# Two recurrent layers on one core: the second layer's first group of input products in the two-level scheme, after the first layer's third group, with other places in the queues

## The chip, the cores and the metric

One Trainium2 chip, one of its cores. The engines of the core work side by side, each on its own queue in order: TensorE (PE, matrix products), VectorE (DVE), ScalarE (ACT), GpSimd (POOL) and SyncE (SP, which only issues DMAs). The metric is the device time of one execution in microseconds (us). Before the change the median of three runs was 1619.63 us (1619.02 to 1619.73); less is better.

## The reference, cut to what matters

Two recurrent layers run over 128 steps, each followed by a residual addition. The batch is 128 rows, a row has 512 features, everything is float32.

```python
def _L0_cond_ref(h_t, z, W, b, alpha):
    Wh = W[:, :D]; Wz = W[:, D:]; leak = 1.0 - alpha
    def step(h, z_t):
        gate = jax.nn.sigmoid(h @ Wh.T + z_t @ Wz.T + b)
        h_new = jnp.tanh(h * leak + gate * z_t)
        return (h_new, h_new)
    ...
def _L1_cond_ref(x, h0, Wx, Wh, b):
    xw = jnp.einsum('ntd,dh->nth', x, Wx) + b
    def step(prev_h, xw_t):
        next_h = jnp.tanh(xw_t + prev_h @ Wh)
        return (next_h, next_h)
    ...
x = x + _L0_cond_ref(cond_1024, x, L0_cond_W, L0_cond_b, L0_cond_alpha)
x = x + _L1_cond_ref(x, cond_1024, L1_cond_Wx, L1_cond_Wh, L1_cond_b)
```

The state products `h @ Wh` come one step after the other. The input products `z @ Wz` and `x @ Wx` do not depend on the state, so they can be formed for many steps at once.

## The kernel before, in words

**Tiling.** Features lie on the 128 partitions in four chunks, the batch of 128 in the free dimension. Layer 0 is "a" in the names of tiles, layer 1 is "b". Layer 1 runs `LAG` = 13 steps behind layer 0, in the same loop: step t holds layer 0's step t and layer 1's step t - 13. A state product of one half of the features (`state_product`, L424) is eight matmuls of 128 columns; a step of both layers has four such halves.

**Input products.** They are formed for groups of 8 steps (`B`) in Strassen's scheme in Winograd's form. On one level (the cases in `FLAT`) a group is 7 products ("outer" 1 to 7) of 4 matmuls with 512 columns, L344. On two levels each of the 7 is split again into 7 leaves: 49 matmuls with 256 columns, L350, in two sweeps, 4 leaves for each outer product in sweep 0 and 3 in sweep 1 (`INNER`). Before the change layer 0's first full group ("a", 1) and layer 1's first group ("b", 0) are on one level, and all later groups are on two.

**What a two-level group needs.** (1) Sums of inputs `S56`, `S73` (`add_up`, on POOL, 8 operations). (2) Nested sums of these, tiles `N12`, `N56`, `N73`, `N4` and `D...` (`nest`, on DVE, 16 operations L210). (3) Combined weights, "leaves": formed once by POOL (`combine_leaves`), written to DRAM (`keep_leaves`, four DMAs for each outer product), and streamed back through ten buffers by SP (`stream`, one DMA for each outer product and sweep, 256 KB or 192 KB; tiles `wsa`, `wsb`). (4) After each outer product `collect` (L371 on ACT for the first use of a part, L373 on DVE for the others) takes it out of its PSUM set (`A` or `B`), since the next but one outer product accumulates into the same set. (5) Between the sweeps eight additions (`gather`, L379, on DVE). Seeds for the state products are then copied into PSUM by ACT (`seed`, L413).

**The plan.** The program is written by a planner in the kernel's own code. `spread` gives each outer product a step, `shape_of` sets the order within a step, and a clock with a fixed cost for each piece gives every PE instruction a time. Everything else is then placed on a lane (DVE, ACT, POOL, SP) at the first free time after what it needs (`place`, `task`, `issue`), and the program is recorded in the order of these times. Each engine executes its queue strictly in that order, and what was placed late by the plan stands late in the queue whatever the real times are.

**x and the results.** A step's x comes by four DMAs on SP (`load_x`, L98), is turned by DVE (`prepare_x`, L168) into one of the T tiles, and a finished step is turned back (`to_natural`, L173) and stored by four DMAs on SP (`store`, L103). There are five x buffers and three o buffers. In a step of layer 0, ACT forms the gate (L471), DVE multiplies and adds (`mix0`, L477 and L480), ACT takes the tanh (L485), POOL adds the residual (L488); layer 1's tanh is L497 on ACT.

**Lines that the change and the prediction touch.** `FLAT` L200, `make` L238, `nest` L305, `set_of` L324, `part` L355, the spreads L531 to L546, `shape_of` L548, the loop over steps L572, the loads of x L786 to L791, the combined weights L794 to L803, the sums of groups L816 to L852, the fills L854 to L870.

Of the kernel before, what the change touches and what calls it, by code (L numbers as in the profile page):

```python
# [43 lines left out]
def kernel(  # L44
# [18 lines left out]
    G = 4  # L63
# [135 lines left out]
    FRESH = 1, 2, 5  # L199
    FLAT = {("a", "flat"): 2, ("a", 1): 4, ("b", 0): 4}  # L200

# [24 lines left out]
    class Layer:  # L226
# [11 lines left out]
        def make(self, what):  # L238
            pool, tag, shape = {"w": (tpool, "T", [P, C, C, P]), "wc": (bpool, "A1", [P, 4, 2, 2, P])}[what]
            setattr(self, what, pool.tile(shape, F32, tag=tag, name=f"{what}{self.name}"))  # L240

# [62 lines left out]

        def nest(self, key, pair, which):  # L305
            n = 1 if pair == "4" else 2
            if (key, pair) not in self.inner:
                self.inner[key, pair] = npool.tile([P, n, 3, 2 * P], F32, tag="N", name=f"N{pair}{self.name}_{key}")
                self.third[key, pair] = dpool.tile([P, n, 2 * P], F32, tag=f"D{pair}", bufs=1 if pair == "4" else 2, name=f"D{pair}{self.name}_{key}")
            i, d = self.inner[key, pair], self.third[key, pair]  # L310
            sums(
                nc.vector, lambda j: d if j == 3 else i[:, :, j - 5],
                lambda b, a: self.quarter(key, pair, b, a), which,
            )
# [9 lines left out]
        def set_of(self, key, sweep, outer):  # L324
            turned = (self.name, key) == ("a", 1) or ((self.name, key) not in FLAT and sweep == 0)
            return "AB"[(outer in (2, 5, 3)) != turned]
# [28 lines left out]
        def part(self, key, i):  # L355
            if key == "flat":
                if key not in self.parts:
                    self.parts[key] = bpool.tile([P, 2, 4, 2 * P], F32, tag="A1", name="Aflat")
                return self.parts[key][:, :, 2 * i : 2 * i + 2]
            if (key, i) not in self.parts:  # L360
                pool, tag = (apool, f"A0{self.name}") if i == 0 else (bpool, "A1")
                self.parts[key, i] = pool.tile([P, 2, 4, 2 * P], F32, tag=tag, name=f"A{i}{self.name}_{key}")
            return self.parts[key, i]
# [166 lines left out]

    spread(2, L0, 1, [(0, 1)], [(0, 2)], [(0, 6)], [(0, 5)], [(0, 3)], [(0, 7)], [(0, 4)])  # L531
    LOOSE = (
# [6 lines left out]
    )  # L539
    for g in range(NB):  # L540
        if g:
            spread(B * g + B, L1, g, *(LOOSE if g == NB - 1 else STEADY))
        else:
            spread(B, L1, 0, [(0, 1)], [(0, 2), (0, 6)], [(0, 5)], [(0, 7), (0, 3)], [(0, 4)])
        if 2 <= g:
            spread(B * g - G, L0, g, *STEADY)  # L546

    def shape_of(t, n):  # L548

        first = ["0", "0"] if t < T else []  # L550
        second = ["1", "1"] if LAG <= t < T + LAG else []
        if not n:
            return first + second
        if t == T:
            return ["u"] + second + ["u"] * (n - 1)
        if t % B < G or not second or not first:
            if t % G == 2 and second and first:
                return first + ["1", "u", "1"] + ["u"] * (n - 1)
            return first + second + ["u"] * n
        if t % G == 2:  # L560
            return first + ["1", "u", "1"] + ["u"] * (n - 1)
        if t % B == B - 1:
            return first + ["u"] * (n - 1) + second + ["u"]
        if t % G == 3:
            return first + ["u"] * n + second
        return first + ["u"] * min(n, 2) + second + ["u"] * max(0, n - 2)
# [3 lines left out]
    start = []  # L570
    clock = BEGIN
    for t in range(T + LAG):  # L572
        start.append(clock)
        left_ = list(units[t])
        halves = {"0": 0, "1": 0}
        u = t - LAG
# [3 lines left out]
        for kind in shape_of(t, len(left_)):  # L580
            if kind == "u":
# [4 lines left out]
                pe[layer.name, key, s, o] = clock  # L586
            elif kind == "0":
                i = halves["0"]
                halves["0"] += 1
                at(clock, L0.state_product, t, i, h0)  # L590
                clock += HALF
                pe["0", t, i] = clock
# [26 lines left out]
    done = {}  # L619
    VEC, LAT = 0.08, 0.065  # L620

# [19 lines left out]
    lanes.take("DVE", 0.0, 25.6)  # L641
    lanes.take("ACT", 0.0, 25.6)


# [87 lines left out]
    for u in range(T):  # L732
        for i in range(2):
# [4 lines left out]
            if u % B == 0:  # L738
                needs += [("c", "b", u // B, 1 if u else 0, 3 if i else 2)]
            task(("seed1", u, i), needs, "ACT", 0.3, 0.39, L1.seed, u, i)  # L740
        if u < T - 1:
            task(("res1", u), [("tanh1", u, 0), ("tanh1", u, 1)], "POOL", 1.27, 1.3, residual, u, h1)
    for key_ in list(pe):
        if len(key_) == 4:
# [3 lines left out]
            if s == 0 and o in COPIED:  # L748
                task(("c", *key_), [("pe", *key_)], "ACT", 0.09 + 0.00083 * n, 0.18 + 0.00083 * n, layer.collect, key, s, o)
            else:  # L750
                task(("c", *key_), [("pe", *key_)], "DVE", *vec(n), layer.collect, key, s, o)
# [9 lines left out]

    def nested_sums(layer, key, what, ok, outers):
        if len(pairs_done) >= 2:
            ok = max(ok, pairs_done[-2] + 0.1)
        occ, dur = vec(256 if what == "4" else 512)
        e = {}
        for which in (5, 7, 6, 3):
            r = max(ok, e.get(5, 0) if which == 6 else 0, e.get(6, 0) if which == 3 else 0) + LAT
            e[which] = place(
                ("N", layer.name, key, what, which), "DVE", r, occ, dur, layer.nest, key, what, which,  # L770
                apart=True,
            )
        pairs_done.append(max(begun[layer.name, key, 0, o] + UNIT[0] for o in outers))
# [12 lines left out]
    for t in turn:  # L786
        if t == 2 * B:
            issue(start[2] + 1.0, 4, load_w1, wx1, "wx")
        landed = issue(max(freed.pop(0) + 0.05, start[max(0, t - 15)] if t > 15 else 0.0), 4, load_x, t) + (5.0 if t < 2 * B else 2.9)
        e = place(("x", t), "DVE", max(landed, start[t - 12] + 0.3 if t >= 2 * B else 0.0), 0.7, 0.71, prepare_x, t)  # L790
        freed.append(e)  # L791


    lanes.take("POOL", 0.0, start[0])  # L794
    issue(start[4] + 1.0, 4, load_w1, wh1, "wh1")
    at(start[3] + 2.0, L1.make, "w")
    for kc in range(C):
        place(("wx", kc), "ACT", start[3] + 2.1, 0.6, 0.7, permute_w1, lambda: L1.w, "wx", kc)
        place(("wh", kc), "ACT", start[7] + 1.0, 0.6, 0.7, permute_w1, lambda: L1.wh, "wh1", kc)
    at(start[7] - 0.02, L1.make, "wc")  # L800
    e = start[7]
    for i in (5, 6, 7, 4):
        e = place(("wc", i), "POOL", e, 1.25, 1.3, L1.combine_weights, i, nc.gpsimd)  # L803

# [11 lines left out]
    for time, name, key in groups:  # L816
        layer = {"a": L0, "b": L1}[name]
        if name == "a":
            have = {t: done["x", t] for t in range(8 * key, 8 * key + 8)}
# [10 lines left out]
        for which, ok in ((5, high), (6, max(high, low)), (7, max(high, low)), (3, low)):  # L830
            for k in range(2):
                ready_ = max(ok, late[PAIR[which][0]] + 0.1, e.get(6, 0.0) if which == 3 else 0.0, e.get(5, 0.0) if which == 6 else 0.0)
                name_ = "S", name, key, which, k
                if (name, key) == ("b", NB - 1):
                    e[which] = place(name_, "DVE", ready_ + LAT, *vec(512), layer.add_up, key, which, nc.vector, k)
                else:
                    e[which] = place(
# [15 lines left out]

    for f in sorted(fill, key=lambda f: f[0]):  # L854
        _, kind, layer, key, what, ok, outers = f
        if kind == 0:
            nested_sums(layer, key, what, ok, outers)
        else:
            occ, dur = vec(512)
            r = ok + LAT  # L860
            for n in range(4):
                name_ = "G", layer.name, key, what, n
                r = place(name_, "DVE", r, occ, dur, layer.gather, key, what, n, nc.vector, apart=True) + 0.04

    for n, o in enumerate((6, 5, 7, 4, 1, 2, 3)):
        e = place(("leaves", o), "POOL", start[0] + 4.0 * n, 1.9, 2.0, L0.combine_leaves, o, nc.gpsimd)
        issue(e + 0.1, 4, L0.keep_leaves, o, nc.sync)
    for n, o in enumerate((6, 5, 7, 4, 1, 2, 3)):
        e = place(("leaves1", o), "POOL", max(e, start[8]), 1.9, 2.0, L1.combine_leaves, o, nc.gpsimd)
        issue(e + 0.1, 4, L1.keep_leaves, o, nc.sync)  # L870

# [41 lines left out]
```

## Time and profile before

| what | value |
|---|---|
| median of three runs | 1619.63 us (1619.02 to 1619.73) |
| the profiled execution | 1619.68 us |
| its span, first to last instruction | 1617.9 us |
| DVE busy | 1197.8 us (74%), 2054 instructions |
| ACT busy | 714.2 us (44%), 1923 instructions |
| POOL busy | 712.7 us (44%), 581 instructions |
| layer state products, PE | 4 groups of 235 to 248 us (L424) |
| x loads on SP | 496 DMAs of 64 KB, median 3.1 us from issue to landing |
| stores on SP | 510 DMAs of 64 KB, 1.8 us |

How to read it: an instruction's row gives its start, its duration, the engine, the line, and the tiles it writes and reads. A matmul in float32 shows as two records, so a state half is 16 records, and a leaf product 2. A row of the timeline joins equal instructions that follow each other without a gap. What lies between 1617.9 and 1619.68 us is outside the first and last instruction.

### The profile page before, as it was taken

The numbers are of one execution on the slowest core, as the hardware profiler recorded it, in microseconds if no ns is written. First come the engines' busy times: TensorE is split into PE (matmuls) and PEld (weight loads), VectorE is DVE, ScalarE is ACT, GpSimd is POOL, SyncE is SP. The second block draws the span as 40 slices with busy tenths as digits, with TensorE's granted clock in tenths as the row PEclk, the third lists the DMA queues.
The fourth block names the chain that finished last, engine by engine and source line by source line (L and its number), as shares of the span: only waits on it lengthen the run. The fifth ranks groups of instructions, "written<-read, shape, count | busy, mean of one in ns | idle before, by whom it ended". The sixth has DMA issues, their size and how long they took to land.

```text
span 1617.9 us, 30816 instructions
## 1 busy us (share of the span) xinstructions
PE 1609.7 (99%) x11340; PEld 1501.8 (93%) x11340; DVE 1197.8 (74%) x2054; ACT 714.2 (44%) x1923; POOL 712.7 (44%) x581
## 2 busy tenths in 40 slices
PE   9999999999999999999999999999999999999998
PEld 8768999999999999999999999999999999999998
DVE  5446787777787777877778877778787787877673
ACT  2444444444444444444444344444444444444444
POOL 5683444424554245442445434454343544434222
PEclk9999999999999999999999999999999999999999
DMA  7643433444434445343453334543345433333133
GB/s 161 184 121 108 126 91 93 106 115 126 115 81 105 105 127 128 79 106 93 126 139 92 99 86 115 139 103 89 94 110 135 118 84 91 93 87 100 42 98 72
DMA packets 218582, 173.18 MB, mean 107 GB/s; under 512 B 24384, under 2 KB 191168, under 8 KB 218432
## 3 DMA queue, kind: packets, MB, share of 16 engines
q1 hardware_dynamic: 214464, 168.59, 40.6%
q10 hardware_dynamic: 3360, 1.57, 0.5%
q8 instruction: 90, 1.47, 0.4%
q0 software_dynamic: 608, 1.06, 0.3%
q14 instruction: 60, 0.49, 0.1%
HBM read 131.14 MB, written 39.98 MB: 106 GB/s over the span
## 4 chain that ended last, share of the span: by engine, by line
PE 99%; DVE 0%; DMA 0%; issue 0%; ACT 0%; ACTq 0%; POOLq 0%; POOL 0%; DVEq 0%
PE r0a L424 14%; PE r1a L424 14%; PE r1b L424 13%; PE r0b L424 13%; PE B_b L350 10%; PE A_b L350 10%; PE B_a L350 9%; PE A_a L350 9%; PE B_a L344 1%; PE A_b L344 1%; PE A_a L344 1%; PE B_b L344 1%; PE r0b L434 1%; PE r0a L445 1%; PE r1b L434 0%; PE r1a L445 0%
## 5 line engine op out<-in xcount | busy, mean ns | idle before, releaser
L488 POOL TENSOR_TENSOR T<-T,h 128x512 f32<-128x512 f32 x254 | 351.7, 1388 | 842.9 <-ACT h L485 652.5
L424 PEld LDWEIGHTS r0a<-h,wha 128*128 128x128 f32 x2032 | 246.5, 192 | 10.6 <-issue 3.3
L424 PE MATMUL r1a<-h,wha 128*128 128x128 f32 x2032 | 247.7, 275 | 0.0
L424 PE MATMUL r0a<-h,wha 128*128 128x128 f32 x2032 | 247.3, 275 | 0.0
L424 PEld LDWEIGHTS r1a<-h,wha 128*128 128x128 f32 x2032 | 237.1, 192 | 0.0
L424 PE MATMUL r0b<-h,whb 128*128 128x128 f32 x1936 | 235.8, 275 | 0.0
L424 PE MATMUL r1b<-h,whb 128*128 128x128 f32 x1928 | 235.0, 275 | 0.0
L424 PEld LDWEIGHTS r0b<-h,whb 128*128 128x128 f32 x1936 | 229.4, 192 | 2.4
L424 PEld LDWEIGHTS r1b<-h,whb 128*128 128x128 f32 x1928 | 227.2, 192 | 1.4
L471 ACT ACTIVATE r0a<-r0a,per_feature 128x128 f32<-128x128 f32 x256 | 87.6, 342 | 296.3 <-PE r0a L424 292.2
L471 ACT ACTIVATE r1a<-r1a,per_feature 128x128 f32<-128x128 f32 x256 | 87.6, 342 | 138.4 <-PE r1a L424 134.3
L497 ACT ACTIVATE h<-r0b,per_feature 128x128 f32<-128x128 f32 x256 | 80.0, 363 | 122.3 <-PE r0b L424 111.5
L477 DVE TENSOR_TENSOR r0a<-r0a,T 128x256 f32<-128x256 f32 x128 | 55.3, 432 | 98.3 <-ACT r0a L471 98.0
L373 DVE TENSOR_TENSOR A0a<-A_a,A0a 128x1024 f32<-128x1024 f32 (+1 forms) x58 | 63.5, 1096 | 74.8 <-PE A_a L350 71.0
L497 ACT ACTIVATE h<-r1b,per_feature 128x128 f32<-128x128 f32 x255 | 79.7, 363 | 86.1 <-PE r1b L424 85.9
L485 ACT ACTIVATE h<-h 128x256 f32<-128x256 f32 x256 | 105.4, 412 | 13.4 <-DVE h L480 13.4
L173 DVE STREAM_TRANSPOSE o<-T 128x512 f32<-128x512 f32 x127 | 87.3, 695 | 26.0 <-POOL T L488 20.2
L168 DVE STREAM_TRANSPOSE T<-x 128x512 f32<-128x512 f32 x128 | 89.4, 701 | 5.6 <-DMA x<-in_x_dram 5.4
L480 DVE SCALAR_TENSOR_TENSOR h<-h,leak,r0a 128x128 f32<-128x128 f32 x254 | 77.0, 345 | 7.5
L480 DVE SCALAR_TENSOR_TENSOR h<-h,leak,r1a 128x128 f32<-128x128 f32 x254 | 77.0, 345 | 4.5
L477 DVE TENSOR_TENSOR r1a<-r1a,T 128x256 f32<-128x256 f32 x128 | 55.4, 433 | 33.6 <-ACT r1a L471 27.2
L373 DVE TENSOR_TENSOR A0b<-A_b,A0b 128x1024 f32<-128x1024 f32 (+1 forms) x60 | 65.4, 1091 | 10.2 <-PE A_b L350 8.1
(253 smaller groups left out, 2885.4 us busy)
## 6 DMA issues: line engine op xcount, KB each, us to landing
out_dram<-o SPq DMA_DIRECT2D x510, 64.0 KB, 1.8
x<-in_x_dram SPq DMA_DIRECT2D x496, 64.0 KB, 3.1
wsb<-leafb SPq DMA_DIRECT2D x105, 256.0 KB, 4.0
wsa<-leafa SPq DMA_DIRECT2D x98, 256.0 KB, 3.5
wsb<-leafb SPq DMA_DIRECT2D x105, 192.0 KB, 3.5
wsa<-leafa SPq DMA_DIRECT2D x98, 192.0 KB, 3.7
leafa<-wla SPq DMA_DIRECT2D x7, 192.0 KB, 2.7
leafb<-wlb SPq DMA_DIRECT2D x7, 192.0 KB, 2.4
```

Of the source, the lines that this page charges most:

```text
L168: nc.vector.transpose(dst.rearrange("p c (a i) -> p c a i", i=S), src.rearrange("p a (c j) -> p c a j", j=S))
L173: nc.vector.transpose(dst.rearrange("p a (c j) -> p c a j", j=S), src.rearrange("p c (a i) -> p c a i", i=S))
L344: nc.tensor.matmul(ps[:, m * n : m * n + n], w[:, c, m, :], a[:, c].rearrange("p t n -> p (t n)"), start=first and c == 0 and m * n % 512 ...
L350: nc.tensor.matmul(ps[:, n], streamed[self.name, key, sweep, outer][:, n], self.left(key, outer, i), start=first and n % 2 == 0, stop=True ...
L373: nc.vector.tensor_tensor(c, sets[tag][:, n], c, ALU.add)
L424: nc.tensor.matmul(banks[m * (len(banks) - 1)][0][:, m], self.wh[:, c, 2 * half + m, :], h[t - 1][:, c], start=alone and n == 0, stop=c == ...
L471: nc.scalar.activation(gate[:, m], gate[:, m], AF.Sigmoid, bias=per_feature[:, 0, f : f + 1])
L477: nc.vector.tensor_tensor(gate, gate, at_of(t)[:, two[i]], ALU.mult)
L480: nc.vector.scalar_tensor_tensor(h0[t][:, f], h0[t - 1][:, f], leak[:, f : f + 1], gate[:, m], ALU.mult, ALU.add)
L485: nc.scalar.activation(h0[t][:, two[i]], h0[t][:, two[i]], AF.Tanh)
L488: (eng or nc.gpsimd).tensor_tensor(at_of(t)[:, part], at_of(t)[:, part], h[t][:, part], ALU.add)
L497: nc.scalar.activation(h1[t][:, f], ps[:, m], AF.Tanh, bias=per_feature[:, 2, f : f + 1])
```

## The change

- ("b", 0) is taken out of `FLAT`, so layer 1's first group is formed on two levels (49 leaves in place of 7 products of 4 matmuls). Its products move from steps 8 to 12 to steps 11 to 14.
- Layer 0's third group ("a", 2) moves from steps 12 to 15 to steps 6 to 10. Layer 0's ("a", 1) is spread over steps 2 to 6 in place of 2 to 8, ("b", 1) takes the new spread `SECOND` at steps 16 to 19, and steps 9, 10, 13, 14 and 15 have an order of their own (`SHAPES`), in which a "+" may bring the next step's state half forward.
- A new helper `either` places an operation on DVE, or on POOL where DVE would end after the operation's due time and POOL would end earlier. Nested sums, gathers, ("b", 0)'s sums and layer 1's combined weights and leaves go through it.
- The load of x is placed for 3.2 us ahead of a time `early`, which for most steps is 0.3 us after the start of step t - 12; before, the load was free to go from the start of step t - 15, and only its turning waited for step t - 12.
- Layer 1's combined weights and its leaves are made before ("b", 0)'s sums; leaves of both layers are made in the order of `OUTER`; `wh1` is loaded four steps later; some parts have other homes (`part`, `make`).

```diff
-    FLAT = {("a", "flat"): 2, ("a", 1): 4, ("b", 0): 4}
+    FLAT = {("a", "flat"): 2, ("a", 1): 4}
...
+            if what == "wc" and self.name == "b":
+                pool, tag = apool, "A0b"
...
-        def nest(self, key, pair, which):
+        def nest(self, key, pair, which, eng):
...
-            turned = (self.name, key) == ("a", 1) or ((self.name, key) not in FLAT and sweep == 0)
+            turned = (self.name, key) not in FLAT and sweep == 0
...
+                pool, tag = {("a", 2, 0): (bpool, "A1"), ("b", 0, 1): (apool, "A0a")}.get((self.name, key, i), (pool, tag))
...
-    spread(2, L0, 1, [(0, 1)], [(0, 2)], [(0, 6)], [(0, 5)], [(0, 3)], [(0, 7)], [(0, 4)])
+    spread(2, L0, 1, [(0, 1)], [(0, 2)], [(0, 6), (0, 5)], [(0, 7), (0, 3)], [(0, 4)])
+    spread(
+        6, L0, 2, [(0, 1)], [(0, 2), (0, 6), (0, 5)], [(0, 7), (0, 3), (0, 4)],
+        [(1, 1), (1, 2), (1, 6), (1, 5)], [(1, 7), (1, 3), (1, 4)],
+    )
+    spread(
+        11, L1, 0, [(0, 1), (0, 2)], [(0, 6), (0, 5), (0, 7), (0, 3), (0, 4)],
+        [(1, 1), (1, 2), (1, 6), (1, 5), (1, 3), (1, 7)], [(1, 4)],
+    )
+    SECOND = (
+        [(0, 1), (0, 2)], [(0, 6), (0, 5), (0, 7), (0, 3)], [(0, 4), (1, 1), (1, 2), (1, 6)], [(1, 5), (1, 7), (1, 3), (1, 4)],
+    )
...
-    for g in range(NB):
-        if g:
-            spread(B * g + B, L1, g, *(LOOSE if g == NB - 1 else STEADY))
-        else:
-            spread(B, L1, 0, [(0, 1)], [(0, 2), (0, 6)], [(0, 5)], [(0, 7), (0, 3)], [(0, 4)])
-        if 2 <= g:
+    for g in range(1, NB):
+        spread(B * g + B, L1, g, *(SECOND if g == 1 else LOOSE if g == NB - 1 else STEADY))
+        if g > 2:
             spread(B * g - G, L0, g, *STEADY)
+    SHAPES = {
+        9: "0uu0uu",
+        10: "0u0uu",
+        13: "0uu0u1u+u+u1",
+        14: "+1u1",
+        15: "011",
+    }
...
+    def either(name, release, n, fn, *args, ops=1, due=0.0):
+        occ, dur = vec(n)
+        occ, dur, slow = occ * ops, dur * ops, POOL_OCC * n * ops
+        s = lanes.find("DVE", release, occ, True)
+        z = lanes.find("POOL", release + 0.03, slow, False)
+        if s + dur > due and z + slow < s + dur:
+            return place(name, "POOL", release + 0.03, slow, slow + 0.05, fn, *args, nc.gpsimd)
+        return place(name, "DVE", release, occ, dur, fn, *args, nc.vector, apart=True)
...
-        landed = issue(max(freed.pop(0) + 0.05, start[max(0, t - 15)] if t > 15 else 0.0), 4, load_x, t) + (5.0 if t < 2 * B else 2.9)
-        e = place(("x", t), "DVE", max(landed, start[t - 12] + 0.3 if t >= 2 * B else 0.0), 0.7, 0.71, prepare_x, t)
+        early = 0.0 if t < 2 * B else 0.0 if t < 2 * B + G else start[4] + 1.0 if t < 3 * B else start[t - 12] + 0.3
+        landed = issue(max(freed.pop(0) + 0.05, early - 3.2), 4, load_x, t) + (5.0 if t < 2 * B else 2.9)
+        e = place(("x", t), "DVE", max(landed, early), 0.7, 0.71, prepare_x, t)
...
-    issue(start[4] + 1.0, 4, load_w1, wh1, "wh1")
-    at(start[3] + 2.0, L1.make, "w")
+    issue(start[8] + 1.0, 4, load_w1, wh1, "wh1")
+    at(start[3] + 0.9, L1.make, "w")
...
+    for n, o in enumerate(OUTER):
+        e = place(("leaves", o), "POOL", start[0] + 4.0 * n, 1.9, 2.0, L0.combine_leaves, o, nc.gpsimd)
+        issue(e + 0.1, 4, L0.keep_leaves, o, nc.sync)
...
+        if (name, key) == ("b", 0):
+            e = max(done["wx", kc] for kc in range(C)) + LAT
+            at(e, L1.make, "wc")
+            for i in (5, 6, 7, 4):
+                e = either(("wc", i), e, 512, L1.combine_weights, i)
+            for o in OUTER:
+                e = either(("leaves1", o), e, 128, L1.combine_leaves, o, ops=4)
+                issue(e + 0.1, 4, L1.keep_leaves, o, nc.sync)
...
-                r = place(name_, "DVE", r, occ, dur, layer.gather, key, what, n, nc.vector, apart=True) + 0.04
+                ok = either(("G", layer.name, key, what, n), ok + LAT, 512, layer.gather, key, what, n, due=due)
```

More of the change, by code (lines that the diff above doesn't have):

```diff
@@ L311, in nest @@
             sums(
-                nc.vector, lambda j: d if j == 3 else i[:, :, j - 5],
+                eng, lambda j: d if j == 3 else i[:, :, j - 5],
                 lambda b, a: self.quarter(key, pair, b, a), which,
@@ L539 @@
     )
-    for g in range(NB):
-        if g:
-            spread(B * g + B, L1, g, *(LOOSE if g == NB - 1 else STEADY))
-        else:
-            spread(B, L1, 0, [(0, 1)], [(0, 2), (0, 6)], [(0, 5)], [(0, 7), (0, 3)], [(0, 4)])
-        if 2 <= g:
-            spread(B * g - G, L0, g, *STEADY)
+    for g in range(1, NB):
+        spread(B * g + B, L1, g, *(SECOND if g == 1 else LOOSE if g == NB - 1 else STEADY))
+        if g > 2:
+            spread(B * g - G, L0, g, *STEADY)
+    SHAPES = {
[5 more added lines that the diff above has]
+    }
     def shape_of(t, n):
+        if t in SHAPES:
+            return list(SHAPES[t])
         first = ["0", "0"] if t < T else []
@@ L562, in shape_of @@
         if t % B == B - 1:
-            return first + ["u"] * (n - 1) + second + ["u"]
+            return first + ["u"] * max(1, n - 1) + second + ["u"] * min(1, n - 1)
         if t % G == 3:
@@ L571 @@
     clock = BEGIN
+    halves = {"0": 0}
     for t in range(T + LAG):
@@ L574 @@
         left_ = list(units[t])
-        halves = {"0": 0, "1": 0}
+        halves["1"] = 0
         u = t - LAG
@@ L586 @@
                 pe[layer.name, key, s, o] = clock
-            elif kind == "0":
-                i = halves["0"]
+            elif kind in "0+":
+                t_, i = divmod(halves["0"], 2)
                 halves["0"] += 1
-                at(clock, L0.state_product, t, i, h0)
+                at(clock, L0.state_product, t_, i, h0)
                 clock += HALF
-                pe["0", t, i] = clock
+                pe["0", t_, i] = clock
             elif not tail:
@@ L619 @@
     done = {}
-    VEC, LAT = 0.08, 0.065
+    VEC, LAT, POOL_OCC = 0.08, 0.065, 0.00244
     def vec(n):
@@ L738 @@
             if u % B == 0:
-                needs += [("c", "b", u // B, 1 if u else 0, 3 if i else 2)]
+                needs += [("c", "b", u // B, 1, 3 if i else 2)]
             task(("seed1", u, i), needs, "ACT", 0.3, 0.39, L1.seed, u, i)
@@ L748 @@
             if s == 0 and o in COPIED:
-                task(("c", *key_), [("pe", *key_)], "ACT", 0.09 + 0.00083 * n, 0.18 + 0.00083 * n, layer.collect, key, s, o)
+                task(("c", *key_), [("pe", *key_)], "ACT", 0.09 + 0.00083 * n, 0.18 + 0.00083 * n, layer.collect, key, s, o,
+                    release=start[7] + 0.3 if (name, key, o) == ("a", 2, 1) else 0.0)
             else:
@@ L760, with nested_sums @@
     pairs_done = []
-    def nested_sums(layer, key, what, ok, outers):
+    def nested_sums(due, layer, key, what, ok, outers):
         if len(pairs_done) >= 2:
             ok = max(ok, pairs_done[-2] + 0.1)
-        occ, dur = vec(256 if what == "4" else 512)
         e = {}
@@ L768, in nested_sums @@
             r = max(ok, e.get(5, 0) if which == 6 else 0, e.get(6, 0) if which == 3 else 0) + LAT
-            e[which] = place(
-                ("N", layer.name, key, what, which), "DVE", r, occ, dur, layer.nest, key, what, which,
-                apart=True,
+            e[which] = either(
+                ("N", layer.name, key, what, which), r, 256 if what == "4" else 512, layer.nest, key, what, which,
+                due=(begun[layer.name, key, 1, outers[0]] if which == 3 else due) - 0.05,
             )
@@ L788 @@
             issue(start[2] + 1.0, 4, load_w1, wx1, "wx")
-        landed = issue(max(freed.pop(0) + 0.05, start[max(0, t - 15)] if t > 15 else 0.0), 4, load_x, t) + (5.0 if t < 2 * B else 2.9)
-        e = place(("x", t), "DVE", max(landed, start[t - 12] + 0.3 if t >= 2 * B else 0.0), 0.7, 0.71, prepare_x, t)
+        early = 0.0 if t < 2 * B else 0.0 if t < 2 * B + G else start[4] + 1.0 if t < 3 * B else start[t - 12] + 0.3
+        landed = issue(max(freed.pop(0) + 0.05, early - 3.2), 4, load_x, t) + (5.0 if t < 2 * B else 2.9)
+        e = place(("x", t), "DVE", max(landed, early), 0.7, 0.71, prepare_x, t)
         freed.append(e)
     lanes.take("POOL", 0.0, start[0])
-    issue(start[4] + 1.0, 4, load_w1, wh1, "wh1")
-    at(start[3] + 2.0, L1.make, "w")
+    issue(start[8] + 1.0, 4, load_w1, wh1, "wh1")
+    at(start[3] + 0.9, L1.make, "w")
     for kc in range(C):
[L798 to L803, printed above, removed]
+        place(("wx", kc), "ACT", start[3] + 1.0, 0.6, 0.7, permute_w1, lambda: L1.w, "wx", kc)
+        place(("wh", kc), "ACT", start[9] + 1.0, 0.6, 0.7, permute_w1, lambda: L1.wh, "wh1", kc)
+    for n, o in enumerate(OUTER):
+        e = place(("leaves", o), "POOL", start[0] + 4.0 * n, 1.9, 2.0, L0.combine_leaves, o, nc.gpsimd)
+        issue(e + 0.1, 4, L0.keep_leaves, o, nc.sync)
     ends = []
@@ L835 @@
                     e[which] = place(name_, "DVE", ready_ + LAT, *vec(512), layer.add_up, key, which, nc.vector, k)
+                elif (name, key) == ("b", 0):
+                    e[which] = either(name_, ready_ + LAT, 512, lambda l, y, w, k, eng: l.add_up(y, w, eng, k), layer, key, which, k)
                 else:
@@ L852 @@
         before, before2 = (name, key), before
-    for f in sorted(fill, key=lambda f: f[0]):
-        _, kind, layer, key, what, ok, outers = f
+    for f in sorted(fill, key=lambda f: f[0] - (8.0 if f[1:5] == (0, L1, 0, "12") else 0.0)):
+        due, kind, layer, key, what, ok, outers = f
         if kind == 0:
-            nested_sums(layer, key, what, ok, outers)
+            nested_sums(due, layer, key, what, ok, outers)
         else:
-            occ, dur = vec(512)
-            r = ok + LAT
             for n in range(4):
-                name_ = "G", layer.name, key, what, n
-                r = place(name_, "DVE", r, occ, dur, layer.gather, key, what, n, nc.vector, apart=True) + 0.04
[L865 to L870, printed above, removed]
+                ok = either(("G", layer.name, key, what, n), ok + LAT, 512, layer.gather, key, what, n, due=due)
     for u in range(T - 1):
```

## The prediction

> **What bounds the kernel now.** I read the page first (busy shares and the chain that ended last), then the waits of PE, then timelines of each engine in one stretch of 20 us.
>
> ```profile
> span 1617.9 us, 30816 instructions
> PE 1609.7 (99%) x11340; PEld 1501.8 (93%) x11340; DVE 1197.8 (74%) x2054; ACT 714.2 (44%) x1923; POOL 712.7 (44%) x581
> PE 99%; DVE 0%; DMA 0%; issue 0%; ACT 0%; ACTq 0%; POOLq 0%; POOL 0%; DVEq 0%
> q8 instruction: 90, 1.47, 0.4%
> ```
>
> PE carries the chain for 99% of the span, and the view of PE's waits between 25 and 260 us is empty. Whatever takes PE work away is a gain in full, and any wait that reaches PE is a loss in full: nothing can give it back. So there are two questions: how much PE work goes, and does anything now come late. Two parts of the PE work show the size of the first:
>
> ```profile
> 88.58 3.44 PE B_a L344 x8
> 92.02 3.43 PE A_b L344 x8
> ```
> ```profile
> 465.27 0.59 PE L350 MATMUL B_a<-S73a,wsa 128*128 128x256 f32 x2
> ...
> 466.57 1.95 PE L424 MATMUL r0b<-h,whb 128*128 128x128 f32 x16
> ...
> 478.58 0.60 PE L350 MATMUL B_b<-T,wsb 128*128 128x256 f32 x2
> ...
> 480.31 0.59 PE L350 MATMUL A_b<-T,wsb 128*128 128x256 f32 x2
> ...
> 482.03 0.59 PE L350 MATMUL B_b<-S56b,wsb 128*128 128x256 f32 x2
> ```
>
> A product on one level takes 3.435 us. On two levels its four leaves of sweep 0 take 1.73 us (478.58 to 480.31) and its three of sweep 1 take 1.30 us (465.27 to 466.57).
>
> **The PE work.** Layer 1's first group: 7 x 3.435 = 24.05 us before, 7 x (1.73 + 1.30) = 21.21 us after. With the unrounded starts this is **-2.87 us**, all on the path. Moving ("a", 2), spreading ("a", 1), the "+" and the changed sets move PE work without changing its amount: 0.
>
> **The load of x, the term that decides.** Before, x is loaded about three steps (36 us) before it is turned: the last x DMA is issued at 1371.4 us and the last turning starts at 1407.2. After the change the load is placed 3.2 us ahead of the turning, and in the changed order four DMAs of x(t), t = 36, 44, ... 124, stand on SP directly behind the eight stores of two results, and DVE turns this x just before layer 0's step t - 12. DVE and ACT run in order, so a late x holds the gate product, the sums for h, ACT's tanh, the next seeds, layer 1's tanh, and at the end the copy (`collect`) of the outer product (0,1) out of PSUM set B. PE's product (0,6) accumulates into that set and must wait. Before the change SP, DVE and ACT do the same things in the same place, with an x needed three steps later:
>
> ```profile
> 469.00 3.77 SPq L103 DMA_DIRECT2D out_dram<-o  x8
> 472.81 1.88 SPq L98 DMA_DIRECT2D x<-in_x_dram  x4
> ```
> ```profile
> 568.55 5.53 SPq L103 DMA_DIRECT2D out_dram<-o  x8
> ```
> ```profile
> 467.65 0.70 DVE L210 TENSOR_TENSOR D12b<-T,N12b 128x512 f32<-128x512 f32 x1
> 468.27 1.29 DVE L173 STREAM_TRANSPOSE o<-T 128x512 f32<-128x512 f32 x2
> ```
> ```profile
> 478.78 0.62 ACT L497 ACTIVATE h<-r1b,per_feature 128x128 f32<-128x128 f32 x2 [0.23 <-PE r1b L424]
> 479.44 0.38 ACT L413 COPY r1b<-A1b 128x256 f32<-128x256 f32 x1
> 480.51 1.01 ACT L371 COPY A0b<-B_b 128x1024 f32<-128x1024 f32 x1 [0.70 <-PE B_b L350]
> ```
>
> The budget, with the start of the step's first state half (PE L424 on r0a, 471.43 in the timeline) as zero:
> - PE starts (0,6) at 482.03, +10.60.
> - ACT before it, back to back: tanh 0.30, seed 0.30, layer 1's tanh 0.52, tanh 0.30, two seeds 0.31 each, tanh 0.66 (478.78 to 479.44), seed 0.31, together 3.02; then the copy 1.01 and 0.03 for the semaphore. The first tanh must start by +6.54.
> - DVE before that: turning 0.62, gate product 0.47, two sums 0.60, semaphore 0.03, and 0.1 from landing to start, 1.82. So x must have landed by +4.72.
> - The first store is issued at 469.00, -2.43. In the changed order D12b (0.62 us, 467.65 to 468.27) no longer stands between the collects and the two results, so stores start at -3.05. From first store to x landed there may be 7.77 us.
>
> How long is that stretch? The thirteen places of before where eight stores, an x load and four stores follow each other take, from first issue to the landing of all four: 8.08, 8.66, 7.59, 7.62, 9.45, 7.83, 7.68, 9.36, 7.88, 8.54, 8.36, 7.41, 9.54 us. The short ones are 5.27 us of issuing and 2.1 to 2.8 of landing; in the long ones SP was held at one issue (the stores of 568.55 took 5.53 us, not 3.77). There are 48 issues over 0.8 us, and 44 of them meet a packet of the q8 row above, instruction code at one packet in 18 us, so about every third such stretch is hit whatever the plan. What exceeds 7.77: 0.31, 0.89, 1.68, 0.06, 1.59, 0.11, 0.77, 0.59, 1.77, in all 7.77 us over thirteen; for the twelve places after the change **+7.2 us**. Bounds: at 7.41 everywhere 0, at 9.54 everywhere 12 x 1.77 = 21. I take the measured mix, as the stretch is the same work; a limit off by 0.25 us either way gives 5.4 or 9.6. Before, the same hold-ups cost nothing: three steps of lead cover them.
>
> A rule of the Trainium skill, "DMA: Bandwidth & Descriptors", section "Anatomy of one DMA — SWDGE (gpsimd) path", gives a DMA a fixed 2.0 us and its bytes at 436 GB/s, an estimate of 2.15 us for 64 KB. By it x would land 7.4 us after the first store, this term would be 0 and the time about 1617.8. The rows differ (median 3.1, up to 5.4 us), and they decide.
>
> **Nested sums of ("b", 1).** With `SECOND`, (0,6) stands right behind step 17's four state halves, at +7.15 us, and its first matmul on N56b at +7.58. Layer 0's first sums end at +3.73 (gate product at +2.74, then 0.47 and 0.52). Then a nested sum 0.62, the second gate product and its sums 0.99, two more nested sums 0.62 and 0.68: ready at +6.81, with 0.77 to spare, if POOL is quiet. It is not: it adds up S73b and then the residuals.
>
> ```profile
> 478.30 1.76 DVE L210 TENSOR_TENSOR N56b<-N56b,S56b 128x512 f32<-128x512 f32 x1
> ```
>
> Beside POOL's addition at 478.06 this sum took 1.76 us instead of 0.68. One such meeting makes PE 0.31 us late, two 1.39; none, 0. I take the middle of one and two, **+0.8 us**, once.
>
> The Trainium skill, "Perfetto Trace Analysis", section "Optimizing Scalar/DVE Operations", warns that moving work between these two engines may not help as they share a read port; this speaks against `either`. By it every meeting would cost a full wait, so 1.4 us here, and the total 0.6 us more.
>
> **The ramp.** DVE gains 12 tensor operations and POOL 19 in all. From 85 to 135 us DVE was busy 25.1 and POOL 40.3 of 50 us, and no PE wait showed. Layer 0's leaves were in DRAM at 73.2 us plus 2 to 3 of landing; the first leaf product now starts at 84.9 (the seventh product of ("a", 1) ends there: two more products of 3.44 before it than in step 6 of before), a stream lands in 3.6, so some 5 us are spare. SP's 14 more streams are 14 x 0.47 = 6.6 us, against one idle stretch of 16.9 us at 82.6. `wh1` comes some 38 us later, around 100 us, with its first use in step 13 after 135. The new homes of parts change only who waits for whom; within DVE's idle half. All 0 while this cover holds. If two or three of the new sums meet POOL on the path, each costs 1.08: bounds 0 and 3. Nearer is before's empty list of waits: **+0.2 us**.
>
> **Sum.** 1619.7 (the profiled execution, 1619.68, 0.05 above the median of the runs) - 2.87 + 7.2 + 0.8 + 0.2 = **1625.0 us**, 0.33% slower. A measurement of this kernel tells 0.2% (3.24 us) from no change, so the borders are 1616.4 and 1622.9.
>
> **Rivals.**
> - *x is in time* (not slower). The budget has more room than I find, over 9.5 us from store to landing, so the twelve places cost nothing: 1619.7 - 2.87 + 0.8 = **1617.6**. For it: seven of the thirteen stretches are within 0.1 us of the limit or below, and the plan itself books 4.7 us for an x load. Against it: ACT's row of eleven instructions has no idle time to give.
> - *Only held issues reach PE.* With a limit of 8.7 us three places remain (0.75, 0.66, 0.84): 2.25 x 12/13 = 2.1 and the time 1619.7 - 2.87 + 2.1 + 0.8 = **1619.7**, no change.
> - *The ramp breaks.* Leaves stored in a queue shared with x, and read back, come late: each 1 us of lateness of a leaf at steps 6 to 14 is 1 us of PE. The 5 us of spare are used up when SP falls 5 us behind, as in the stretch of 81 to 99 us before, where it stood 16.9 us for one leaf; a further 3 us late gives **1628**.
> - *The change doesn't do what it says.* 49 matmuls of 256 columns stand in the changed program for ("b", 0); ruled out.
>
> **How the numbers follow.** Forecast 0.55 (its own range 1623 to 1628), x in time 0.22, only held issues 0.15, ramp 0.08. Slower: nine tenths of the first, all of the last and little of the third, 0.60. Faster by over 0.2% would need a gain over 3.24 us, more than PE loses: 0.03. Within: 0.37. The range leaves out a tenth on each side: 1617.5 to 1628.5.
>
> **What would show it.** Right: PE waits in the list of waits at L352, twelve places about 99.6 us apart from some 280 us on, each 0 to 1.8 us; DVE's waits for DMAs of x at L168, about 2 to 4 us each; one PE wait of about a microsecond near 188 us at N56b. The state halves and leaf products as long as before, PE's busy time without waits shorter by 2.9. Wrong: no wait of DVE's gate product behind L168, a copy of B_b that starts as soon as PE is done with (0,1), or PE waits in other steps, above all before 140 us.

## The result: 17 us slower, 1.1%

The changed kernel takes 1636.64 us, the median of five runs (1634.74 to 1640.56), against 1619.6 us before (1619.02 to 1619.73): the ratio is 1.011, 95% interval 1.0095 to 1.0125. The forecast was 1625.0 us with a range of 1617.5 to 1628.5. The side was right, the size was not. The runs also spread by 5.8 us where they spread by 0.7 before.

The profiled execution (1636.64 us) is the median one. First the top of its page, then one of the costliest groups:

```profile
span 1634.8 us, 30798 instructions
PE 1613.9 (99%) x11382; PEld 1508.6 (92%) x11382; DVE 1223.8 (75%) x2066; ACT 713.3 (44%) x1923; POOL 731.6 (45%) x600
...
PE 87%; DVE 3%; SPq 3%; DMA 2%; issue 2%; POOL 2%; ACT 1%; ACTq 0%; POOLq 0%; DVEq 0%
...
L168 DVE STREAM_TRANSPOSE T<-x 128x512 f32<-128x512 f32 x128 | 89.2, 700 | 80.9 <-DMA x<-in_x_dram 80.8
```

PE still has 99% by the page, yet the chain that ended last, on PE for 99% before, is on it for 87% now; the rest runs through SP, the DMAs of x, DVE, ACT and POOL. DVE waited 80.8 us for x in front of its turning. The view of PE's waits, which was empty between 25 and 260 us before, is this:

```profile
PE B_b L352 <- POOL T L491: 6.2, 4, 1.8
PE B_b L352 <- issue: 2.7, 6, 0.8
PE B_a L352 <- DVE A0a L376: 2.7, 2, 1.5
...
PE B_b L352 <- DVE N56b L210: 1.2, 1, 1.2
...
```

The releaser in the first two rows misleads: it is what the profile saw last, and POOL does not release this product. The view gives less than the whole, too, as it leaves out short waits. So I took the time from each matmul record's start to the next one's start in both traces and subtracted the usual distance (0.2156 us with 256 columns, 0.1115 with 128, 0.4293 with 512). The sums of what is over, by stretch of time:

| stretch, us | over in the change, less before | what waits there |
|---|---|---|
| 0 to 40 | -0.2 | nothing new |
| 40 to 60 | 0.7 | state half of step 4, behind ACT |
| 60 to 80 | 0.7 | product (0,6) of ("a", 1), for S56a from POOL |
| 80 to 100 | 2.65 | ("a", 2), for a collect and a nested sum on DVE, and 0.5 of it a state half |
| 100 to 180 | 0.85 | small waits |
| 180 to 200 | 1.5 | ("b", 1), for N56b |
| 200 to 270 | 1.95 | 1.65 of it at 263 us, for a collect on DVE |
| after 270 | 11.6 | product (0,6) of layer 1, eleven of twelve places |
| all | 19.7 | |

The products themselves became shorter as worked out: 98 matmul records of 256 columns more and 56 of 512 columns less are 21.13 - 24.04 = -2.9 us. Together +16.8 us; the span grew by 16.9.

One of the twelve places, as SP, DVE, ACT and PE show it (four timelines, each of one engine):

```profile
374.76 5.08 SPq L103 DMA_DIRECT2D out_dram<-o  x8
379.88 1.89 SPq L98 DMA_DIRECT2D x<-in_x_dram  x4
```
```profile
384.53 0.71 DVE L168 STREAM_TRANSPOSE T<-x 128x512 f32<-128x512 f32 x1 [4.93 <-DMA x<-in_x_dram]
385.17 0.40 DVE L480 TENSOR_TENSOR r0a<-r0a,T 128x256 f32<-128x256 f32 x1
```
```profile
389.00 0.38 ACT L416 COPY r1b<-A1b 128x256 f32<-128x256 f32 x1
389.31 1.01 ACT L374 COPY A0b<-B_b 128x1024 f32<-128x1024 f32 x1
```
```profile
390.42 0.67 PE L352 MATMUL B_b<-S56b,wsb 128*128 128x256 f32 x2 [1.83 <-POOL T L491]
```

The x is issued behind the last stores and lands at 384.34 (+6.52 us after the step's start at 377.82); DVE stood idle for 4.93 us and turns it at 384.53; ACT's row follows without a gap (each copy starts as the one before is through). The copy of B_b starts at 389.31, 11.49 us after the step's start; in the forecast's rows of before it starts 9.08 us after it (480.51 less 471.43). PE begins (0,6) 2.0 us late. This is the chain of the forecast's budget, instruction for instruction.

### The profile page after: what moved, and what is told of

Read it like the earlier page. It is cut to its first block, busy times and chain, and to the rows that moved or that the text cites. A ratio compares the mean times of both kernels' runs of the same rounds, so it can differ in the third digit from the quotient of the medians.

```text
span 1634.8 us, 30798 instructions
## 1 busy us (share of the span) xinstructions
PE 1613.9 (99%) x11382; PEld 1508.6 (92%) x11382; DVE 1223.8 (75%) x2066; ACT 713.3 (44%) x1923; POOL 731.6 (45%) x600
## 4 chain that ended last, share of the span: by engine, by line
PE 87%; DVE 3%; SPq 3%; DMA 2%; issue 2%; POOL 2%; ACT 1%; ACTq 0%; POOLq 0%; DVEq 0%
PE r0a L427 13%; PE r1a L427 12%; PE r1b L427 12%; PE r0b L427 12%; PE B_b L352 10%; PE A_b L352 10%; PE B_a L352 9%; PE A_a L352 8%; DMA x<-in_x_dram 2%; SPq L98 2%; SPq L103 1%; DVE h L483 1%; POOL T L491 1%; PE r0b L437 1%; DVE T L168 1%
## 5 line engine op out<-in xcount | busy, mean ns | idle before, releaser
L491 POOL TENSOR_TENSOR T<-T,h 128x512 f32<-128x512 f32 x254 | 346.2, 1368 | 835.5 <-ACT h L488 647.4
L168 DVE STREAM_TRANSPOSE T<-x 128x512 f32<-128x512 f32 x128 | 89.2, 700 | 80.9 <-DMA x<-in_x_dram 80.8
L376 DVE TENSOR_TENSOR A0b<-A_b,A0b 128x1024 f32<-128x1024 f32 (+1 forms) x64 | 69.2, 1081 | 12.4 <-PE A_b L352 9.2
```

The lines of the kernel that those rows point to most:

```text
L168: nc.vector.transpose(dst.rearrange("p c (a i) -> p c a i", i=S), src.rearrange("p a (c j) -> p c a j", j=S))
L376: nc.vector.tensor_tensor(c, sets[tag][:, n], c, ALU.add)
L491: (eng or nc.gpsimd).tensor_tensor(at_of(t)[:, part], at_of(t)[:, part], h[t][:, part], ALU.add)
```

## The experiments

Ten kernels, in three groups; each group ran on one chip beside the kernel before (1619.22, 1619.27 and 1619.04 us there). Waits are sums as in the table above.

### Is it x, and is it its place in the queue?

**x three steps ahead, as before the change.**

```diff
-        landed = issue(max(freed.pop(0) + 0.05, early - 3.2), 4, load_x, t) + ...
+        landed = issue(max(freed.pop(0) + 0.05, early - 3.2 if t < 3 * B else start[t - 15]), 4, load_x, t) + ...
```

> The changed kernel with one edit: from x of step 24 on, the load may go from the start of step t - 15, as before the change, and only the turning waits for step t - 12. SP still issues an x behind the eight stores, but one that is needed three steps later. Theory A (the late x makes the twelve waits of PE ahead of product (0,6) of layer 1, 11.5 us in the profile, and the wait of 1.7 us at 263 us): all thirteen gone, 1636.6 - 13.2 = 1623.4 us, 1621.5 to 1625. Rival B (these waits come from sums that either puts on POOL and that hold up DVE; x is only where it shows): the twelve waits stay, 1634 us or more. Rival C (x makes half of them): 1628 to 1632.

1623.8 us (1623.28 to 1624.62), 1.0029 of before (1.0018 to 1.0039). After 250 us nothing is over any more. Theory A holds, B and C fall. In this kernel, in the one with one microsecond more of lead and in the first with leaf 6 on POOL, the plan put the fourth addition of layer 1's first `gather` behind the first collect of sweep 1, so steps 2 and 3 of layer 1 get another sum; the number of instructions is the same.

**The same, with the first 20 steps planned exactly as in the change** (`t < 4 * B` in the line above).

> The changed kernel with the load of x free to go from the start of step t - 15, but only from x of step 32 on, so that the first 20 steps are planned exactly as in the change. Theory A: the twelve waits ahead of (0,6) and the one at 263 us go, all else stays as in the changed kernel's profile: 1636.6 - 11.6 - 1.7 = 1623.3 us, 1622 to 1624.5, and what is left over the time before comes from the waits below 200 us, some 7 us, less the 2.9 us of products.

1622.65 us (1622.2 to 1624.9), ratio 1.0022 (1.0013 to 1.0032): as expected. All of the view of PE's waits in this kernel:

```profile
PE r0b_-1_113 L153 <- POOL condT L135: 1.3, 1, 1.3
PE B_b L352 <- DVE N56b L210: 1.1, 1, 1.1
PE r0a L448 <- DVE wa L179: 1.0, 1, 1.0
PE r0a L427 <- ACT r0a L416: 0.7, 2, 0.4
PE r1a L448 <- DVE wa L179: 0.3, 2, 0.2
PE A_a L352 <- DVE A0a L376: 0.2, 1, 0.2
```

No wait of this view after 200 us is left, and the sum of what is over after 270 us is that of the kernel before; the rows of L153 and L448 stand in the first 11 us, where the kernel before waits too. SP still does the same there: eight stores from -3.06 us, an x behind them, and this x lands at +4.55 to +6.18 us after the step's start, over the limit in most places. It costs nothing, since DVE needs it three steps later.

**One microsecond more of lead.**

```diff
-... early - 3.2)
+... early - (3.2 if t < 3 * B else 4.2))
```

> The changed kernel with the load of x placed 4.2 us ahead of its turning in place of 3.2, from step 24 on. This one microsecond puts the four DMAs of the x in question ahead of the eight stores in SP's queue, which waits in front of the first store for its result; they go out some 20 us earlier. Theory A (what decides is that the x stands behind the eight stores): as with three steps of lead, 1623.4 us, 1621.5 to 1625.5, no waits ahead of (0,6). Rival D (only the length of the lead counts, one microsecond buys at most one microsecond in each place): of the twelve waits of 0 to 2.2 us those above 1 keep what is over 1, some 4 us in all, 1627 to 1629.

1625.67 us (1624.71 to 1625.93), ratio 1.0038 (1.0025 to 1.0051), just over the upper end of A's range and below D's. The x of the fences above, on SP and then on DVE:

```profile
355.16 1.85 SPq L98 DMA_DIRECT2D x<-in_x_dram  x4
375.53 6.88 SPq L103 DMA_DIRECT2D out_dram<-o  x12
```
```profile
379.05 0.70 DVE L168 STREAM_TRANSPOSE T<-x 128x512 f32<-128x512 f32 x1
```

It goes out some 20 us ahead of the stores, and DVE does not wait for it. The waits of the twelve places are gone altogether. The one at 263 us stayed, at 2.4 us: there another x of the same kind did not change its place (DVE waited 3.06 us for it). Without it the time would be 1623.3, what three steps of lead gave (1623.8) within 0.5. So one microsecond on the plan's clock was worth 11.6 us, because it moved four DMAs ahead of a store on which SP waits: D falls.

**The kernel before, with the late x alone, and with a slightly later one.**

```diff
-... start[max(0, t - 15)] if t > 15 else 0.0)
+... (start[max(0, t - 15)] if t > 15 else 0.0) if t < 3 * B else start[t - 12] + 0.3 - 3.2)
```

The second kernel has 2.6 in place of 3.2.

> The kernel before with only the load of x placed as in the change (3.2 us ahead of the turning, from step 24 on). Here the x stands behind four stores and not eight, so it lands some 1.9 us less late: from the first store at -2.44 us and 7.8 us of issuing and landing less 1.9, about +3.5 us after the step's start, against a limit of +4.7 measured in the changed kernel. Theory A: only where SP is held at an issue does it pass the limit, five places by 0 to 0.6 us: 1619.6 to 1622. Rival E (a load just in time costs PE in every group of steps, wherever it stands): 1627 or more.

> The kernel before with the load of x placed 2.6 us ahead of the turning in place of 3.2, from step 24 on. The 0.6 us put the x of one step in eight behind eight stores of results in place of four, and other x loads move back by one place too. Theory A (a late x costs when it stands behind the eight stores): landings of the thirteen stretches of before against the limit of +4.7 us after the step's start, 0.3 to 2.4 us in each of twelve groups, 15 us, and waits of PE in the profile behind a late turning of x: 1628 to 1640. Rival D (the lead counts, not the place): 0.6 us less lead costs at most 0.6 us in twelve places over the run with 3.2 us (1619.5), 1619.5 to 1626.7.

With 3.2 us: 1619.53 us, ratio 1.0002 (0.9993 to 1.0012). DVE waits 52.2 us for x in all, PE 0.2 us, in one place. With 2.6 us: 1634.55 us (1634.37 to 1634.88), ratio 1.0095 (1.0078 to 1.0112). In the place that answers to the fence above:

```profile
572.82 5.14 SPq L103 DMA_DIRECT2D out_dram<-o  x8
578.01 1.89 SPq L98 DMA_DIRECT2D x<-in_x_dram  x4
```
```profile
582.35 0.71 DVE L168 STREAM_TRANSPOSE T<-x 128x512 f32<-128x512 f32 x1 [3.27 <-DMA x<-in_x_dram]
582.98 0.40 DVE L477 TENSOR_TENSOR r1a<-r1a,T 128x256 f32<-128x256 f32 x1
```

Eight stores, x, and DVE idle, in a kernel that has nothing else of the change. A load 3.2 us ahead is free in the kernel before (E falls), with 0.6 us less it is not, and single waits of PE reach 1.2 us, twice the lead given up (D falls here too). The 15 us did not come as expected, though: PE's waits ahead of (0,6) are only 4.0 us, in seven places, as this x stands in front of the second half of the step alone (L477 on r1a above, r0a in the change). The waits ahead of (0,3) and (0,4), a step further on, come to some 8.5 us. In this group they follow the next x, which stands behind four stores and not eight (DVE waited 1.27 us for it at 594.6). So the number of stores is not the rule: what costs is an x that lands after its turning is due, where DVE, ACT and PE have no time to spare behind it. The run shows this mechanism and not its price in the changed kernel. It also shows that waits of DVE for x are no measure: they are 53.9 us in all here and 52.2 in the run that lost nothing.

### What makes PE wait in the ramp

**Layer 1's input weights loaded earlier**, by 4 us in the plan and 4.5 us in the trace (issued at 40.61 in place of 45.13; on top of x three steps ahead from step 32).

```diff
-            issue(start[2] + 1.0, 4, load_w1, wx1, "wx")
+            issue(start[2] - 3.0, 4, load_w1, wx1, "wx")
```

> The same, and the four DMAs of layer 1's input weights stand two x loads (8 DMAs) earlier in SP's queue. In the change ACT's first copy of these weights stands ahead of the gate of layer 0's step 3 and waited 2.3 to 3.8 us for the DMA; the gate, and by it the next state half on PE, came late. Theory H (this wait makes PE's waits at 56 us, 0.2 to 1.8 us, and makes DVE late for the waits of 60 to 100 us): the copy's wait goes, PE's waits between 40 and 60 us fall to 0.1, those of 60 to 100 us shrink by a part, and the time falls by 0.7 to 2.5 us, to about 1621.5. Rival I (the copies themselves, 0.6 us each, are in the gate's way, landed or not): 0.3 us or less.

1622.43 us (1621.7 to 1624.07), 0.2 us less than without: within the spread, so the time alone says nothing for H, and I would give it as well. The trace tells them apart. ACT in the changed kernel, then here:

```profile
53.08 0.62 ACT L185 COPY wb<-wx_in 128x512 f32<-128x512 f32 x1 [2.26 <-DMA wx_in<-in_L_cond_Wx_dram]
53.60 0.71 ACT L474 ACTIVATE r0a<-r0a,per_feature 128x128 f32<-128x128 f32 x2
```
```profile
50.42 0.62 ACT L185 COPY wb<-wx_in 128x512 f32<-128x512 f32 x1
51.30 0.72 ACT L474 ACTIVATE r0a<-r0a,per_feature 128x128 f32<-128x128 f32 x2 [0.25 <-PE r0a L427]
```

In the change the copy of the weights stands ahead of the gate of step 3 and waits for its DMA, and the gate waits behind it. Here it waits for nothing, the gate starts as PE is done, and PE's waits between 40 and 60 us fall from 1.07 us (without this edit) to 0.02, those of 60 to 80 from 0.72 to 0.35: H is right about these. But those of 80 to 100 us rise from 1.48 to 2.68: PE comes to the first product of ("a", 2) 1.4 us sooner, and the collect that it waits for only 0.3 us sooner (it starts at 84.64 in place of 84.95), as DVE reaches the sums ahead of it only 0.4 us sooner. The gain was given back.

**Layer 1's third leaf on POOL**, once with x three steps ahead alone, once with the weights earlier too.

```diff
-                e = either(("leaves1", o), e, 128, L1.combine_leaves, o, ops=4)
+                e = place(("leaves1", o), "POOL", e, 1.9, 2.0, L1.combine_leaves, o, nc.gpsimd) if o == 6 else either(...)
```

> The changed kernel with x loaded three steps ahead, and the four sums of layer 1's third leaf (outer product 6) on POOL in place of DVE. In the changed kernel these four took 1.20 to 1.35 us each on DVE at 79.35 to 84.4 us, beside POOL's additions, against 0.28 us each for those at 77.3; behind them on DVE stand the nested sums and the collect for which PE waits at 85.5 to 89.1 and 96.6 us (1.34 + 0.43 + 0.13 + 0.33). Theory F (the meetings of DVE and POOL over small sums make these waits): PE's waits between 80 and 100 us fall from 2.6 to under 0.7 us and the time is 1.5 to 2.5 us below that of the kernel with x three steps ahead alone, about 1621.3. Rival G (x of steps 20 to 23, for which DVE waits at 63 to 68 us, makes DVE late): no change of these waits, the same time within 0.7 us.

> The same as the run with the weights loaded earlier, and the sums of layer 1's third leaf on POOL in place of DVE. Theory F (the meeting of DVE and POOL over small sums makes the waits of 80 to 100 us): these waits go for good now that DVE isn't late from before, another 1.0 to 2.5 us, about 1620. Rival J (what DVE no longer does, POOL does, and DVE meets it later at the same price, as in the run with x three steps ahead and this leaf on POOL, where a wait of 1.8 us appeared at 95 us): no gain, within 0.7 us.

1622.94 us (1622.19 to 1624.0) against 1623.8, and 1621.45 us (1620.37 to 1622.27) against 1622.43: 0.9 and 1.0 us less, short of F's expectation and above J's. The waits at 84 to 89 us went, and a new one of 1.75 us came at 93 to 95 us, ahead of a collect. The sums of 80 to 100 us went from 1.51 to 1.88 us in the first pair, where F expected under 0.7, and from 2.68 to 1.87 in the second, which gave 0.8 back between 180 and 200 us. So the two profiled executions of the second pair are equally long, and the traces do not show where the 1 us of the medians comes from: the waits moved, as J has it.

**Leaf 5 on DVE too: the suspected cost doubled** (with the weights earlier, and leaf 6 on DVE as in the change).

```diff
+                e = place(("leaves1", o), "DVE", ...) if o == 5 else either(("leaves1", o), ...)
```

> The suspected cost doubled: weights loaded earlier, leaf 6 on DVE as in the change, and leaf 5's four small sums behind it on DVE too, in place of POOL. Theory F: beside POOL's additions these four take 1.2 us each, not 0.28; the nested sum and the collect behind them come up to 4.8 us later, and PE's wait at 84 us grows from 1.35 to between 2.5 and 6 us: 1623.5 to 1627. By their own length alone (4 x 0.28) it would be 1.1 us more: 1623.5. Rival G (the wait at 84 us has another cause, an x or a stream that comes late): it stays at 1.35, 1622.4.

1625.85 us (1625.34 to 1627.12), 3.4 us more than without; PE's waits of 80 to 100 us rise from 2.68 to 6.03. DVE's timeline in this kernel:

```profile
76.74 0.29 DVE L220 TENSOR_TENSOR wlb<-wb,wlb 128x128 f32<-128x128 f32 x1
...
78.08 0.28 DVE L220 TENSOR_TENSOR wlb<-wcb 128x128 f32<-128x128 f32 x1
78.40 1.38 DVE L220 TENSOR_TENSOR wlb<-wcb,wlb 128x128 f32<-128x128 f32 x1
79.70 1.35 DVE L220 TENSOR_TENSOR wlb<-wcb 128x128 f32<-128x128 f32 x1
80.98 1.35 DVE L220 TENSOR_TENSOR wlb<-wcb,wlb 128x128 f32<-128x128 f32 x1
82.25 1.35 DVE L220 TENSOR_TENSOR wlb<-wcb 128x128 f32<-128x128 f32 x1
83.63 1.24 DVE L220 TENSOR_TENSOR wlb<-wcb,wlb 128x128 f32<-128x128 f32 x1
...
85.46 1.21 DVE L376 TENSOR_TENSOR A0a<-B_a,A0a 128x1024 f32<-128x1024 f32 x1
```
```profile
78.37 1.27 POOL L210 TENSOR_TENSOR S73a<-T,T 128x512 f32<-128x512 f32 x1 [5.09 <-DMA leafb<-wb]
79.59 1.31 POOL L491 TENSOR_TENSOR T<-T,h 128x512 f32<-128x512 f32 x1
80.87 1.31 POOL L210 TENSOR_TENSOR S73a<-T,T 128x512 f32<-128x512 f32 x1
```

The same small sum takes 0.28 us until POOL starts an addition at 78.37, and 1.24 to 1.38 us while POOL's five additions last, one for each; POOL's hardly grow here (1.27 to 1.31). The collect behind them (85.46) is what PE waits for at 85.3 us; its longer wait after that, of 2.5 us, is for a nested sum that stands further back in the same queue. Theory F holds for these waits and G falls.

**Leaves 3 and 4 later, and on POOL**, where the plan then puts them by itself (with the weights earlier and leaf 6 on POOL).

```diff
+                if o in (3, 4):
+                    e = max(e, start[7] + 3)
```

> Weights loaded earlier, leaf 6 on POOL, and the leaves 3 and 4 of layer 1 not before 3 us into step 7; there POOL is free and takes them, so that DVE sheds eight more small sums, which in the run before stood at 84.4 to 88.0 us ahead of the nested sums and of the collect for which PE waited 1.75 us at 93 us. Theory F (what counts is what DVE has ahead of a collect, at the price of a meeting): the wait at 93 us goes, 1621.45 - 1.7 = 1619.8 us, 1619 to 1620.5. Rival J (the meetings only move): a new wait of over 1 us between 95 and 115 us, 1621 or more.

1620.53 us (1620.25 to 1621.72), ratio 1.0009 (1.0000 to 1.0018), 0.9 us less than with the weights earlier and leaf 6 on POOL, in place of 1.7: just over F's range, below J's. Nothing is over between 80 and 100 us (0.02), but 0.84 us appears at 102 us, at a collect behind sums that now meet POOL's leaves, and 0.6 us between 40 and 60 us, where ACT's copy waits for nothing but DVE is late with `mix0`: it waited 1.37 us for an x at 51.8 us. So a late x has a part in the ramp as well. This is the best version found; it is still 1.5 us behind the kernel before.

## Why the forecast was wrong

The time is 11.6 us over the forecast. By the sums of waits, the ramp makes 4.7 us of it, the size of the x term 4.4, a place outside the twelve 1.7, and the nested sums 0.6.

- **The PE work** (-2.87 us): right, -2.9 by the count of matmuls, and the durations did not change.
- **The load of x** (+7.2 us): the mechanism, the place, the number of places and the way through DVE, ACT and the copy were right; the rivals "x is in time" and "only held issues reach PE" fell. The size was too small: 11.6 us. In the place shown the first store was issued at -3.06 us after the step's start (I had -3.05). The limit from first store to landing was not 7.77 but 7.58 to 7.65 us: so much is a stretch less the wait it made, in all eleven places that waited. In the fences above the turning starts 0.19 us after x has landed (I had 0.1) and PE 0.10 us after the copy (I had 0.03). The stretches were longer than those of before, 7.58 to 9.61 with a mean of 8.51 us against 8.31; that part looks like chance, as the run with x three steps ahead from step 32 has 8.31 again. Place by place the limit makes 1.8 us and the stretches 1.9; a first matmul record 0.1 us slower behind each wait makes the rest. Six at most of the thirteen stretches of before were within about 0.1 us of the forecast's limit or below, not seven, so it spoke less for "x is in time" than I had it. The estimate of 2.15 us for a load, which left this term at 0, comes from a section on DMAs that GpSimd issues, and these go out on SP: the last of each four landed 2.2 to 3.7 us after its issue in the twelve places. I had worked out that 0.25 us in the limit moves the term by 2.4 us, and had not let the range follow it together with a change of the stretch.
- **"Twelve places"** left one out: the 1.65 us at 263 us is an x too. DVE waited 1.44 us for it, ran without a gap from there to the collect, and the wait went with three steps of lead. It stands behind other transfers than the twelve, and the forecast had no place for it.
- **Nested sums of ("b", 1)** (+0.8 us): 1.37 us in the changed kernel, 1.24 to 1.4 in the runs. Both sums that I named met POOL (1.70 and 1.75 us each); I had worked out 1.39 for two meetings and then taken the middle of one and two. The wait stays with x three steps ahead, so x does not make it.
- **The ramp** (+0.2 us): this step failed. 4.9 us came between 40 and 180 us. "All 0 while this cover holds" rested on how busy the engines are on average and on SP's queue; no stream of leaves was late (each landed 7.9 us or more before its first product, 9.0 or more below 200 us, where I had reckoned with 5 to spare), so the rival "the ramp breaks" was right about the place and wrong about the mechanism. What I had not followed are two queues: ACT's, where the copies of layer 1's weights moved ahead of a gate (`start[3] + 2.1` to `start[3] + 1.0`) while their DMA came no sooner (issued at 45.38 us, before at 44.29), and DVE's, where 0.28 us of work became 1.3 because POOL was adding. An engine that is half idle on average was full from 78.2 us on, up to the collect at 86.0 for which PE waited.

The Trainium skill, "SBUF — State Buffer", section "Who interferes with whom", says that DVE and GpSimd share one pair of ports as an exclusive lock; its section "SBUF: two separate sides" adds that whichever starts first has the pair for its whole instruction and the other is blocked. The rows of the run with leaf 5 on DVE agree: what is paid is POOL's addition, 1.27 us, however short DVE's own sum is.

What stays open: no experiment was aimed at the waits at 60 us and between 100 and 180 us (some 1.6 us together) or at those for N56b; that POOL causes them is read from the rows alone. Whether the two-level ("b", 0) can bring its 2.9 us is open as well: the runs took 16 us of the loss away, and the waits in the ramp that remain, about 5 us, are more than the gain.

## What to carry to other kernels

A load placed just in time is priced at its place in the queue: ask what stands directly ahead of it and whether the queue waits there, since a microsecond on the planner's clock can decide whether eight DMAs stand in front; and where the engines behind it have no time to spare, each place pays for the last of its landings, in every round. When work moves earlier on an engine in order, look at what it waits for and at who stands behind it now, on every queue and also where the engine has idle time on average. Small sums on VectorE beside long GpSimd additions cost one addition each (1.24 to 1.38 us for 0.28 here), so look for a stretch where nothing that TensorE waits for stands behind them; here moving them took one wait away and made another.

## What was not expected of the hardware

In the run with leaf 5 on DVE, PE waited twice with one matmul, two records, between (three timeline rows of PE, then two stretches of the view by windows: length, busy time of PE, PEld, DVE, ACT and POOL, the granted clock, the DMA share and GB/s):

```profile
86.72 0.70 PE L352 MATMUL B_a<-T,wsa 128*128 128x256 f32 x2 [1.43 <-DVE A0a L376]
89.96 2.93 PE L352 MATMUL B_a<-N12a,wsa 128*128 128x256 f32 x6 [2.54 <-DVE N12a L210]
92.68 0.58 PE L427 MATMUL r0a<-h,wha 128*128 128x128 f32 x2
```
```profile
84.00:88.00 4.00, 1.99 (x6) 0.52 (x4) 3.90 (x8) 0.00 (x0) 3.84 (x7) 1.00 0.54 139
88.00:93.00 5.00, 3.04 (x8) 2.50 (x9) 4.96 (x10) 2.39 (x6) 4.92 (x8) 0.67 0.00 2
```

The six records took 2.93 us in place of 1.46 (so long take the six on N12b in the changed kernel), at a mean granted clock of 0.67 in this stretch (0.50 from 89.7 to 93.0 us). The waits cost 1.4 us more than their own length. After the single waits of up to 2.0 us in the changed kernel only the first record is slower, by 0.1 us. The Trainium skill, "TensorE: Matmul & The Clock Gate", section "What's actually happening", has the array at half its clock once it was idle for a window of about 3.4 us. The half pace agrees (2.93 against 1.46); the idle time here was 1.4 and 2.5 us with two records between, neither as long as that by itself.
